# Attention: the order of the gate, sum and context transfers on one DMA queue

## The chip, the cores and the metric

The kernel runs on one core of a Trainium2 chip. The metric is the device time of one execution in microseconds (us), and the median of several runs is given. A profile of one further execution records every instruction on the engines: TensorE (PE, with its weight loads as PEld), VectorE (DVE), ScalarE (ACT) and GpSimd (POOL). It also records the issue of every transfer on SyncE's queue (SP). All the transfers this text speaks of are issued on SP, one after the other.

## The reference

The input x has 128 sequences of 64 tokens and 128 channels, in float32. Four blocks are applied one after the other; three of them hold attention with 16 heads of 8 channels:

```python
def _attend(q, k, v):
    attn = jnp.einsum('bhnd,bhsd->bhns', q, k) * SCALE
    attn = jax.nn.softmax(attn, axis=-1)
    o = jnp.einsum('bhns,bhsd->bhnd', attn, v)
...
x = x + g_sa * (_attend(q, k, v) @ sa_proj_w + sa_proj_b)      # self: gated per sequence
x = x + (_attend(q_, k_, v_) @ ca_proj_w + ca_proj_b)          # cross: keys, values of the context
x = x + g_ff * (gelu(xm @ fc1_w + fc1_b) @ fc2_w + fc2_b)      # MLP
```

Block 0 is self-attention, cross-attention to `ctx_1024` and an MLP. Block 1 is one cross-attention with modulated inputs. Block 2 is again self-attention, cross-attention and an MLP. Block 3 is an attention to 64 prototypes, a router and three experts. Gates, shifts and scales come from `cond_1024`, one row per sequence.

## The kernel before

The tokens are cut into 16 groups of 512 (8 sequences). x stays in SBUF as 16 tiles `xs[s]` of 128 tokens x 4 x 128 channels. There are five attention stages, called L0s and L2s (self), L0c, L1c and L2c (cross). A pair of a stage and a group is an item here, so there are 80 items: 32 of self-attention and 48 of cross-attention. L0s and L0c are one stream of 32 items, and L1c, L2s and L2c are another of 48; between and behind the streams run the MLPs and block 3.

The program order on each engine is written out by hand. `prepare` and `finish` are generators, and `step(k)` advances them by single pieces; each item i has two steps, u = 0 and u = 1, one for each half of its sequences. In a step DVE takes the maxima of the scores (`mx`, L449) and subtracts them (`e`, L451), PE turns the result, ACT takes the exponential (`eT`, L471), PE weighs the values, and ACT copies the outcome into `o` (L492).

`prepare` of an item has eight pieces. The first loads the context tile `c` (256 KB, L363) for a cross item and does nothing for a self item; the later ones make the statistics, the normed input `xn` (POOL), the normed context `cn`, and then keys, queries and values. `step` calls the first piece of item i + 4 at the start of the step with u = 0. In L0c the transposed context is also stored to DRAM (`ctxT`, L385).

`finish` of item j has four pieces:

1. In step (j + 1, u = 1): for a self item, four loads of the gate tiles `gt` (128 KB each, L505); four stores of the rows of `o` that hold the sums of the softmax to DRAM (`sums`, L510); one load `rc` (L515) that brings the sums back spread over 128 partitions; four transfers within SBUF that move half of `o` (L518).
2. In step (j + 2, u = 0): DVE's reciprocal of `rc` (L520), its store to DRAM (`recs`, L522), and the load `rb` (256 KB, L524) that broadcasts it to all channels.
3. In step (j + 2, u = 1): on POOL `oT` = `o` x `rb` (L527) and the addition of the bias to x (L529), which is `gt[1]` for a self item.
4. In step (j + 3, u = 0): the projection `py` on PE (L533), and for a self item `y` = `py` x `gt[0]` on DVE (L538) and its addition to x on POOL (L539); for a cross item one addition on DVE (L535).

SP works through its queue in that order. A transfer that waits for a semaphore holds all those behind it. `rc` waits until `sums` has landed, `recs` waits for the reciprocal, and `rb` waits until `recs` has landed. `o`, `gt` and `rc` have two buffers each, `rb` and `oT` one, `c` three.

Of the kernel before, what the change touches and what calls it, by code (L numbers as in the profile page):

```python
# [9 lines left out]
F32 = mybir.dt.float32  # L10
# [10 lines left out]
NT = TT * P  # L21
# [38 lines left out]
def tile_kernel(ctx: ExitStack, tc: tile.TileContext, a: dict, out: bass.AP):  # L60
    nc = tc.nc
# [4 lines left out]
    def const(shape, name):  # L66
        return cp.tile(shape, F32, tag=name, name=name)
# [38 lines left out]
    for name, n in (("L0_xcond_ca_proj_b", P), ("L1_xcond_bp", P), ("L2_xcond_b_cproj", P), ("L3_xcond_router_b", 3)):  # L106
        t = const([P, n], name)
# [16 lines left out]
    dp = ctx.enter_context(tc.tile_pool(name="dp", bufs=1, space=bass.MemoryType.DRAM))  # L124
# [307 lines left out]
    def scores(pools, at, u):  # L432

        pool, psc = pools[0], pools[2]
        qT, kbd = at["qT"], at["kbd"]

        sc = psc.tile([P, 4, 512], F32, tag="sc", name="sc")
        for t2 in range(2):
            for h in range(2):
                b = 4 * u + 2 * t2 + h  # L440
                for g in range(4):
                    T.matmul(  # L442
                        sc[ts(h, L), g, ts(t2, 256)],
                        qT[ts(g, 32), ts(b, L)],
                        kbd[ts(g, 32), :, b, :],
                        start=True, stop=True,
                    )
        mx = pool.tile([P, 32], F32, tag="mx", name="mx")
        V.tensor_reduce(mx, sc.rearrange("p g (m k) -> p (g m) k", k=L), AX.X, ALU.max)  # L449
        e = pool.tile([P, 32, L], F32, tag="e", name="e")  # L450
        V.tensor_tensor(  # L451
            e, sc.rearrange("p g (m k) -> p (g m) k", k=L),
            mx.unsqueeze(2).broadcast_to([P, 32, L]), ALU.subtract,
        )
        return e

    def turned(pools, e, eT, gg):

        pp = pools[3].tile([P, 2, 512], F32, tag="pt", name="pp")
        e6 = e.rearrange("p (g t i j) k -> p g t i (j k)", g=4, t=2, i=2)
        for g2 in range(2):
            for i in range(2):
                for t2 in range(2):
                    for h in range(2):
                        T.transpose(  # L467
                            pp[:, h, ts(4 * g2 + 2 * i + t2, L)],
                            e6[ts(h, L), 2 * gg + g2, t2, i], ident[ts(h, L), ts(h, L)],
                        )  # L470
        S.activation(eT[:, gg], pp, AF.Exp, scale=HD ** -0.5)  # L471

    def weighted(pools, at, u, eT):


        pool, psum = pools[:2]
        po = psum.tile([P, 2, 256], F32, tag="mm", name="po")
        e7 = eT.rearrange("p a h (g i t q) -> p a h g i t q", g=2, i=2, t=2)

        for i in range(2):  # L480
            for t2 in range(2):
                for h in range(2):
                    for g in range(4):
                        T.matmul(  # L484
                            po[ts(g, 32), i, ts(2 * t2 + h, L)],
                            at["vbd"][:, 4 * u + 2 * t2 + h, 2 * g + i, :],
                            e7[:, g // 2, h, g % 2, i, t2, :],
                            start=True, stop=True,
                        )
        if u == 0:  # L490
            at["o"] = pool.tile([P, 2, NT], F32, tag="o", name="o")
        S.copy(at["o"][:, :, ts(u, 256)], po)  # L492

    def finish(pools, at):

        pool, psum = pools[:2]
        s, o = at["s"], at["o"]
        cross = at["layer"][2] == "c"
        if not cross:
            gt = []  # L500
            for i in range(2):
                t = pool.tile([P, TT, P], F32, tag=f"gt{i}", name="gt")
                for h in range(2):
                    r = gates[at["wp"]][i].rearrange("(s t h) c -> s h t c", t=TT, h=2)[s, h]
                    nc.sync.dma_start(t[ts(h, L)], r.unsqueeze(0).broadcast_to([L, TT, P]))  # L505
                gt.append(t)

        sums = dp.tile([16, NT], F32, tag="sums", name="sums", bufs=2)
        for g in range(4):
            nc.sync.dma_start(  # L510
                sums[ts(g, 4), :].rearrange("(i j) t -> j i t", i=2),
                o[32 * g + 16 : 32 * g + 18, :, :],
            )
        rc = pool.tile([P, L], F32, tag="rc", name="rc")
        nc.sync.dma_start(rc, sums.rearrange("h (c t) -> (h c) t", t=L))  # L515

        for g in range(4):
            nc.sync.dma_start(o[32 * g + 16 : 32 * g + 32, 0, :], o[32 * g : 32 * g + 16, 1, :])  # L518
        yield
        V.reciprocal(rc, rc)  # L520
        recs = dp.tile([16, NT], F32, tag="recs", name="recs", bufs=2)
        nc.sync.dma_start(recs.rearrange("h (c t) -> (h c) t", t=L), rc)  # L522
        rb = pool.tile([P, NT], F32, tag="rb", name="rb", bufs=1)
        nc.sync.dma_start(rb, recs.unsqueeze(1).broadcast_to([16, HD, NT]))  # L524
        yield
        oT = pool.tile([P, NT], F32, tag="oT", name="oT", bufs=1)
        G.tensor_tensor(oT, o[:, 0, :], rb, ALU.mult)  # L527
        bias = proj_bias[at["wp"]].unsqueeze(1).broadcast_to([P, TT, P]) if cross else gt[1]
        G.tensor_tensor(xs[s], xs[s], bias, ALU.add)  # L529
        yield  # L530
        py = psum.tile([P, TT, P], F32, tag="mm", name="py")
        for t in range(TT):
            T.matmul(py[:, t, :], oT[:, ts(t, P)], w[at["wp"]][:, 0], start=True, stop=True)  # L533
        if cross:
            V.tensor_add(xs[s], xs[s], py)  # L535
        else:
            y = pool.tile([P, TT, P], F32, tag="y", name="y")
            V.tensor_tensor(y, py, gt[0], ALU.mult)  # L538
            G.tensor_tensor(xs[s], xs[s], y, ALU.add)  # L539

    def attend(pools, ats):

        n = len(ats)
        prep = [prepare(pools, at) for at in ats]
        fin = [finish(pools, at) for at in ats]

        def go(gens, i):
            if 0 <= i < n:
                next(gens[i], None)

        def ahead(*which):
            for i in which:
                go(prep, i)


        halves = [dict(at=at, u=u) for at in ats for u in range(2)]

        def step(k):
            i, u = divmod(k, 2)
            now, last, past = (  # L560
                halves[k - d] if 0 <= k - d < 2 * n else None for d in range(3)
            )
            if u == 0:
                go(prep, i + 4)
            if now:
                now["e"] = scores(pools, now["at"], now["u"])
            if last:
                last["eT"] = pools[0].tile([P, 2, 2, 512], F32, tag="eT", name="eT")
                turned(pools, last["e"], last["eT"], 0)
            if past:  # L570
                weighted(pools, past["at"], past["u"], past["eT"])
            if u == 0:
                go(fin, i - 2)
                go(prep, i + 1)
                go(fin, i - 3)
            else:
                go(prep, i + 1)
            if last:
                turned(pools, last["e"], last["eT"], 1)
            if u == 0:  # L580
                go(prep, i + 2)
                go(prep, i + 3)
            else:
                go(prep, i + 1)
                go(prep, i + 2)
                go(fin, i - 1)
                go(fin, i - 2)
                go(prep, i + 4)

        return ahead, [lambda k=k: step(k) for k in range(2 * n + 5)]  # L590

    def attention_of(s, layer):
# [628 lines left out]
```

## Time and profile before

| | us |
|---|---|
| median of 3 runs | 1682.3 |
| lowest, highest | 1681.4, 1682.74 |
| the profiled execution | 1678.51 |
| its span, first to last instruction | 1676.7 |
| PE busy | 1598.2 |
| DVE busy | 1287.6 |
| ACT busy | 1030.9 |
| POOL busy | 1069.9 |
| TensorE clock granted, mean share of full | 0.993 |

L0s runs from about 40 to 250 us of the span, L0c to about 430, L1c from about 590 to 790, L2s to about 1000 and L2c to about 1185. A line of a group of instructions gives the line of the kernel, the engine, the operation, output and inputs, and after the first bar the busy time in us and the mean of one in ns; after the second bar stands the idle time of the engine before these instructions, with what ended it behind the arrow. A line of a timeline gives the start and duration in us, the engine and the line; a bracket at its end gives the engine's idle time before it and what ended that. `SPq` is the issue of a transfer by SP's queue, not the transfer itself.

### The profile page before, as it was taken

The numbers are of one execution on the slowest core, as the hardware profiler recorded it, in microseconds if no ns is written. First come the engines' busy times: TensorE is split into PE (matmuls) and PEld (weight loads), VectorE is DVE, ScalarE is ACT, GpSimd is POOL, SyncE is SP. The second block draws the span as 40 slices with busy tenths as digits, with TensorE's granted clock in tenths as the row PEclk, the third lists the DMA queues.
The fourth block names the chain that finished last, engine by engine and source line by source line (L and its number), as shares of the span: only waits on it lengthen the run. The fifth ranks groups of instructions, "written<-read, shape, count | busy, mean of one in ns | idle before, by whom it ended". The sixth has DMA issues, their size and how long they took to land.

```text
span 1676.7 us, 64398 instructions
## 1 busy us (share of the span) xinstructions
PE 1598.2 (95%) x27552; PEld 1071.5 (64%) x27552; DVE 1287.6 (77%) x2426; ACT 1030.9 (61%) x1696; POOL 1069.9 (64%) x1816
## 2 busy tenths in 40 slices
PE   6999989999899899999999899998999999999998
PEld 4666667777554467767767667776555566666665
DVE  6999879999555599999999889998354566666665
ACT  4877757776433578778787778886334444444442
POOL 4777766677699978886778777675745233344322
PEclk8999999999999999999999999999999999999999
DMA  7233333232211012212333332221200011111100
GB/s 218 66 88 80 91 109 96 82 90 63 64 32 54 26 50 65 60 47 54 83 91 88 94 91 66 67 60 46 85 1 7 27 38 39 35 36 38 30 13 16
DMA packets 154812, 104.14 MB, mean 62 GB/s; under 512 B 36069, under 2 KB 133279, under 8 KB 154527
## 3 DMA queue, kind: packets, MB, share of 16 engines
q1 hardware_dynamic: 154320, 100.01, 21.6%
q8 instruction: 216, 3.54, 0.9%
q14 instruction: 69, 0.57, 0.1%
q10 hardware_dynamic: 207, 0.03, 0.0%
HBM read 75.60 MB, written 13.89 MB: 53 GB/s over the span
## 4 chain that ended last, share of the span: by engine, by line
PE 66%; DVE 17%; DMA 6%; SPq 4%; POOL 3%; issue 2%; ACT 2%; POOLq 0%; DVEq 0%; ACTq 0%
PE sc L442 7%; DVE mx L449 7%; DVE e L451 7%; PE pp L467 6%; PE ph L994 6%; PE ph L995 6%; PE ph L651 6%; PE py L657 5%; PE po L484 5%; PE po L1025 5%; PE psT L311 4%; PE py L533 3%; PE pvv L423 3%; PE pq L414 3%; PE pk L401 3%
## 5 line engine op out<-in xcount | busy, mean ns | idle before, releaser
L471 ACT ACTIVATE eT<-pp 128x1024 f32<-128x1024 f32 x320 | 329.6, 1030 | 175.1 <-PE pp L467 174.9
L449 DVE TENSOR_REDUCE mx<-sc 128x32 f32<-128x2048 f32 x160 | 366.1, 2288 | 50.3 <-PE sc L442 50.3
L451 DVE TENSOR_TENSOR e<-sc,mx 128x2048 f32<-128x2048 f32 x160 | 366.7, 2292 | 5.5
L467 PEld LDWEIGHTS pp<-ident,e 64*128 64x128 f32 x5120 | 185.5, 140 | 140.3 <-ACT eT L471 40.8
L467 PE MATMUL pp<-ident,e 64*128 64x64 f32 x5120 | 229.4, 230 | 6.3 <-DVE e L451 4.7
L409 POOL TENSOR_SCALAR kbd<-kT,mask 128x512 f32<-128x512 f32 x318 | 214.5, 693 | 30.1 <-ACT kT L403 27.4
L341 POOL TENSOR_SCALAR xn<-x,nmu,rs 128x128 f32<-128x128 f32 x504 | 220.0, 450 | 13.2
L527 POOL TENSOR_TENSOR oT<-o,rb 128x512 f32<-128x512 f32 x80 | 102.1, 1276 | 189.4 <-DMA rb<-recs 52.5
L442 PE MATMUL sc<-kbd,qT 32*64 32x256 f32 x5120 | 181.9, 391 | 20.6 <-DVE e L451 20.0
L652 ACT ACTIVATE h<-ph,vec 128x512 f32<-128x512 f32 x128 | 87.4, 688 | 158.8 <-PE ph L651 158.7
L484 PE MATMUL po<-eT,vbd 128*32 128x64 f32 x10240 | 177.7, 221 | 4.6 <-DVE y L538 4.0
L1001 ACT ACTIVATE h<-h 128x512 f32<-128x512 f32 x112 | 69.1, 628 | 160.4 <-DVE h L997 130.8
L484 PEld LDWEIGHTS po<-eT,vbd 128*32 128x32 f32 x10240 | 151.4, 110 | 17.6 <-DVE y L538 4.8
L299 POOL TENSOR_TENSOR rs<-rs,nhalf 128x4 f32<-128x4 f32 x128 | 130.4, 1018 | 10.7
L442 PEld LDWEIGHTS sc<-kbd,qT 32*64 32x64 f32 x5120 | 99.4, 132 | 57.0 <-issue 25.1
L997 DVE TENSOR_TENSOR h<-ph,ab 128x512 f32<-128x512 f32 x112 | 76.9, 687 | 64.4 <-PE ph L995 64.3
L492 ACT COPY o<-po 128x512 f32<-128x512 f32 x160 | 95.6, 598 | 28.3 <-POOL oT L527 11.1
L289 DVE BATCH_NORM_STATS2 st<-x 128x6 f32<-128x128 f32 x512 | 110.3, 278 | 0.0
L994 PE MATMUL ph<-nx,w 128*128 128x512 f32 x192 | 99.8, 601 | 0.0
L1018 POOL TENSOR_SCALAR g<-g 128x512 f32<-128x512 f32 x16 | 10.0, 625 | 140.4 <-ACT g L1017 140.4
L1025 PEld LDWEIGHTS po<-w_2o,h 128*128 128x128 f32 x768 | 92.2, 192 | 10.9 <-issue 8.4
L1025 PE MATMUL po<-w_2o,h 128*128 128x128 f32 x768 | 96.4, 275 | 1.8 <-ACT h L1001 1.8
(253 smaller groups left out, 2884.6 us busy)
## 6 DMA issues: line engine op xcount, KB each, us to landing
rb<-recs SPq DMA_DIRECT2D x80, 256.0 KB
c<-in_ctx_dram SPq DMA_DIRECT2D x80, 256.0 KB
o<-o SPq DMA_DIRECT2D x320, 32.0 KB
gt<-gate_L_xcond_sa_proj_w SPq DMA_DIRECT2D x64, 128.0 KB
gt<-gate_L_xcond_W_proj SPq DMA_DIRECT2D x64, 128.0 KB
sums<-o SPq DMA_DIRECT2D x320, 8.0 KB
x<-in_x_dram SPq DMA_DIRECT2D x16, 256.0 KB
ctxT<-cm SPq DMA_DIRECT2D x16, 256.0 KB
```

The lines of the kernel that those rows point to most:

```text
L289: V.bn_stats(st[:, t, :], src[:, t, :])
L299: G.tensor_tensor(rs, rs, nhalf, ALU.pow)
L341: engine.tensor_scalar(xn[:, t, :], src[:, t, :], nmu[:, t : t + 1], rs[:, t : t + 1], ALU.add, ALU.mult)
L409: (V if at.get("first") and j % 2 else G).tensor_scalar(kbd[:, j], by_batch(kT), mask[:, j : j + 1], 1.0, ALU.mult, ALU.mult)
L442: T.matmul(sc[ts(h, L), g, ts(t2, 256)], qT[ts(g, 32), ts(b, L)], kbd[ts(g, 32), :, b, :], start=True, stop=True,)
L449: V.tensor_reduce(mx, sc.rearrange("p g (m k) -> p (g m) k", k=L), AX.X, ALU.max)
L451: V.tensor_tensor(e, sc.rearrange("p g (m k) -> p (g m) k", k=L), mx.unsqueeze(2).broadcast_to([P, 32, L]), ALU.subtract,)
L467: T.transpose(pp[:, h, ts(4 * g2 + 2 * i + t2, L)], e6[ts(h, L), 2 * gg + g2, t2, i], ident[ts(h, L), ts(h, L)],)
L471: S.activation(eT[:, gg], pp, AF.Exp, scale=HD ** -0.5)
L484: T.matmul(po[ts(g, 32), i, ts(2 * t2 + h, L)], at["vbd"][:, 4 * u + 2 * t2 + h, 2 * g + i, :], e7[:, g // 2, h, g % 2, i, t2, :], start=T ...
L994: T.matmul(ps, wn, d["nx"], start=True, stop=False)
L1025: T.matmul(po[:, ex, :], d[q][:, ts(t, P)], k3["w_2o"][:, q, :], start=r == 0, stop=r == 1)
```

## The change

In the first piece of `finish` the four stores of `sums` are issued ahead of the four loads of `gt` instead of behind them; the load `rc` and the rest follow as before. In `step`, the first piece of `prepare` of item i + 4, that is the load of `c`, is called behind the second piece of `finish` of item i - 2 instead of at the start of the step. On SP's queue it then stands behind `recs` and `rb` of that item instead of in front of them. Nothing is added or taken away.

```diff
@@ finish
         cross = at["layer"][2] == "c"
+
+        sums = dp.tile([16, NT], F32, tag="sums", name="sums", bufs=2)
+        for g in range(4):
+            nc.sync.dma_start(
+                sums[ts(g, 4), :].rearrange("(i j) t -> j i t", i=2),
+                o[32 * g + 16 : 32 * g + 18, :, :],
+            )
+
         if not cross:
             gt = []
             for i in range(2):
...
                 gt.append(t)
-
-        sums = dp.tile([16, NT], F32, tag="sums", name="sums", bufs=2)
-        for g in range(4):
-            nc.sync.dma_start(
-                sums[ts(g, 4), :].rearrange("(i j) t -> j i t", i=2),
-                o[32 * g + 16 : 32 * g + 18, :, :],
-            )
         rc = pool.tile([P, L], F32, tag="rc", name="rc")
@@ step
-            if u == 0:
-                go(prep, i + 4)
             if now:
                 now["e"] = scores(pools, now["at"], now["u"])
...
             if u == 0:
                 go(fin, i - 2)
+                go(prep, i + 4)
                 go(prep, i + 1)
                 go(fin, i - 3)
```

## The prediction

> **What bounds the kernel now.** I read the page first: it names the busy engines.
>
> ```profile
> PE 1598.2 (95%) x27552; PEld 1071.5 (64%) x27552; DVE 1287.6 (77%) x2426; ACT 1030.9 (61%) x1696; POOL 1069.9 (64%) x1816
> ```
>
> No share of the whole span decides here, because the change touches only the five attention stages. So I went to the groups of instructions on DVE, first in the window 71 to 250 us (14 items of the first self-attention stage, L0s), then in 785 to 1000 us (L2s).
>
> ```profile
> L520 DVE RECIPROCAL rc<-rc 128x64 f32<-128x64 f32 x14 | 7.7, 551 | 16.7 <-DMA rc<-sums 16.7
> ...
> L520 DVE RECIPROCAL rc<-rc 128x64 f32<-128x64 f32 x17 | 9.3, 549 | 13.5 <-DMA rc<-sums 13.5
> ```
>
> The number after the second bar is idle time of DVE before the group: 16.7 and 13.5 us, all waiting for rc to land. Apart from its waits for PE in front of `mx` (7.1 and 8.8 us) and 1 us before `e`, DVE is never idle in those windows. An item costs DVE 4 x 2.29 (mx, e) + 0.55 + 0.63 (y) + 1.23 (statistics) = 11.6 us, and a self item that does not stall takes 11.9 us from one end of its second o copy to the next (71.45, 83.36, 95.24, 107.13). The stalls are therefore time of the kernel.
>
> Why is rc late? The timeline of SP's queue over one stalled item of L2s shows one closed loop:
>
> ```profile
> 954.43 3.45 SPq L505 DMA_DIRECT2D gt<-gate_L_xcond_W_proj  x4
> 957.97 1.34 SPq L510 DMA_DIRECT2D sums<-o  x4
> 961.06 0.34 SPq L515 DMA_DIRECT2D rc<-sums  x1
> 961.45 2.46 SPq L518 DMA_DIRECT2D o<-o  x4
> 963.95 0.59 SPq L363 DMA_DIRECT2D c<-in_ctx_dram  x1
> 964.58 0.50 SPq L522 DMA_DIRECT2D recs<-rc  x1
> 968.58 0.56 SPq L524 DMA_DIRECT2D rb<-recs  x1
> 969.26 2.88 SPq L505 DMA_DIRECT2D gt<-gate_L_xcond_W_proj  x4
> 972.26 1.31 SPq L510 DMA_DIRECT2D sums<-o  x4
> ```
>
> The columns are start and duration of the issue. The only pauses are two round trips, sums to rc (1.75 us) and recs to rb (3.5 us). ACT and DVE for the same item:
>
> ```profile
> 965.32 0.59 ACT L492 COPY o<-po 128x512 f32<-128x512 f32 x1 [0.28 <-PE po L484]
> ...
> 963.00 0.55 DVE L520 RECIPROCAL rc<-rc 128x64 f32<-128x64 f32 x1 [2.54 <-DMA rc<-sums]
> ...
> 976.83 0.55 DVE L520 RECIPROCAL rc<-rc 128x64 f32<-128x64 f32 x1 [2.23 <-DMA rc<-sums]
> ```
>
> The o that sums reads was ready at 965.91, but sums was issued at 972.26: 6.35 us late, because SP was still waiting for recs and then issued gt. From sums to sums the loop is 14.29 us, more than the 11.9 us of the engines. Where c loads are in the loop (the last six items of L0s and of L2s) the items take 12.8 to 15.8 us from oT to oT. Without them SP needs 11 to 13 us and DVE stalls only now and then.
>
> An item that does not stall, also L2s:
>
> ```profile
> 865.88 0.64 ACT L492 COPY o<-po 128x512 f32<-128x512 f32 x1
> 869.26 1.32 SPq L510 DMA_DIRECT2D sums<-o  x4
> 871.97 0.34 SPq L515 DMA_DIRECT2D rc<-sums  x1
> 873.96 0.54 DVE L520 RECIPROCAL rc<-rc 128x64 f32<-128x64 f32 x1
> ```
>
> From the end of o (866.52) to the place that the reciprocal has in DVE's order is 7.44 us. A chain from o to landed rc that is shorter than this costs DVE nothing.
>
> **The change part by part.**
>
> Gate loads behind sums (32 self items). Nothing is added; four issues of gt (3.0 us for four on average, 2.6 to 3.7) change places with four of sums (1.32 us). SP waits between sums and rc for the sums to land: 1.63 us on average in the self items. Now gt is issued in that wait, so the loop gets shorter by about 1.6 us, and when SP is the late one, sums starts 3.0 us sooner. rc, though, comes behind gt: sums 1.32 + 0.1 + gt 3.0 + 0.1 = 4.5 us after sums starts instead of about 3.0. Net, rc is 1.5 us sooner where SP is late, and up to 1.5 us later where SP has been waiting for o. Queued behind rc on SP are the four o shuffles, recs and rb; all move with it. The consumers of gt, the add on POOL (L529) and y on DVE (L538), come after rb has landed, that is over 13 us after o; gt gets there in about 8.
>
> What rc itself takes when it stands behind 512 KB of gt is not in this trace. Lower bound: 1.67 us from issue to reciprocal, the least now, with nothing in front of it. Upper bound: gt's last load lands as late as the slowest rb (239.45 to oT at 244.41, 4.96 us), and rc with it. rc's issue starts 0.72 us after that load's, so 4.2 us. I take 2.2, near the lower end, because sums stands directly behind gt today and takes only 1.63 us to land against 1.2 us at best without gt (1044.47 to 1045.69): 0.4 us more. The chain is then 4.5 + 2.2 = 6.7 us, inside the 7.44. With gt at 3.7 it is 7.4, still just inside.
>
> The c load behind rb (48 cross items are loaded in this way; 12 of the loads fall in self items). Issue 0.59 us, 256 KB. It stood before recs and now stands behind rb, ahead of the next sums and, in L0c and the end of L0s, ahead of the store ctxT. SP loses no work. From recs to rb the self items take 2.4 to 4.2 us where c stands just before recs (mean 3.1) and mostly 1.76 without c, now and then over 3 (mean 2.3): 0.9 us of the loop. The next sums now stands behind c's data; its landing may take longer (bound below 0, above the 0.9 that c costs recs now), but gt's 3.0 us of issue cover a landing of 1.63 + 0.9. c itself arrives 5 to 6 us later. Its nearest reader, cn of L2c, runs 14.2 us after the issue (1062.04 to 1076.23), so some 8 us are left. In the cross stages the reciprocal does not wait (o end 1043.28 to reciprocal 1051.20 is 7.9 us, and rc, issued at 1045.69, has 5.5 us for a landing of 1.7), and the items run at 12.0 us with PE busy 108.00 of 108.00 us (window 1031 to 1139). There an earlier rb gains nothing. A gain is at most 1 us (13 periods of L0c, 254.84 to 411.82, are 157.0 us against 156.0 at 12.0). A loss needs a sums more than 1.4 us later at the tightest item (rc at 332.11, reciprocal at 335.21), and c can delay it by 0.9. I take 0.
>
> The new loop with c: sums 1.34 + 0.1 + gt 3.0 + 0.1 + rc 0.39 + o 2.82 + recs 0.35 + wait 1.8 + rb 0.68 + c 0.63 = 11.2 us, and 11.8 with ctxT in L0s. It is below 11.9, but in L0s only just.
>
> The sum: DVE's stalls of 16.7 + 13.5 = 30.2 us go, less what comes back where a loop of 11.8 us has a slow issue or a slow landing. I keep 4 us for that (0.35 us for each of 12 items with c). A second count agrees: from the o end of the third item of L0s (71.45) to that of the first of L0c (254.84) are 14 periods, 183.4 us against 166.5 at 11.89; in L2s 805.07 to 994.40 are 15 periods, 189.3 against 178.4. That is 16.9 + 11.0 = 27.9 us, and it includes a granted clock of 0.79 in the window 240 to 250 us, where PE stands idle for 2.68 us before py at 246.34. So 26 us. The profiled execution took 1678.5 us (span 1676.7 and 1.8 around it), 3.8 below the median; 1678.5 - 26 = 1652.5, in terms of the median 1656.
>
> **The rivals.**
>
> Slower: rc held behind gt. It decides from the point where the stall is again the 1.0 us that an item loses now (30.2 us over 30 items): chain 8.44, so rc to reciprocal 3.9 us. At the upper bound of 4.2 us with gt at 3.0 the chain is 8.7, a stall of 1.3, +9 us over 30 items: 1692. For it: 512 KB in 512-byte pieces stand in front. Against it: sums lands 1.63 us after standing in the same place. An intermediate form, in which gt's last load lands like the typical rb (3.5 us from its issue, so rc after 2.8) gives a chain of 7.3 us, and 8.0 with gt at 3.7; a quarter of the items then stall 0.6 us, 4.5 us in all: 1660.
> The Trainium skill, page "DMA: Bandwidth & Descriptors", section "Queues, rings and completion order", says that a DMA's completion count is written only after all earlier writes of the same DMA engine; this speaks against the change, since rc could not be reported before gt has landed. By that rule the intermediate form holds at least; the trace, in which sums follows gt with only 0.4 us more, does not settle it.
>
> Half the gain: the wait moves on to POOL. oT (L527) waits for rb, and ACT's o copy two items on waits for oT; the waits of ACT for oT, those put down to gt among them, are 10.1 us in 71 to 250 and 7.9 in 785 to 1000. If they are a limit of their own and stay, 30.2 - 18 = 12 us are gained: 1670. For it: POOL idles 48.0 us before 17 oT in L2s. Against: these waits stand in the same items as the stalls (973.52 waits 1.86 us), and POOL works only 9.7 us per item (its groups of that window added up).
>
> No change: SP is not the limiter after all, sums waits for o as in L1c, and only the order differs: 1682. The 6.35 us above speak against it.
>
> **How the numbers follow.** Forecast 0.53 (its own range 1648 to 1664: all 30.2 us and a little of the clock, down to 18), the intermediate form 0.20, half the gain 0.14, no change 0.03, slower 0.10. The range 1645 to 1674 takes in the forecast, the intermediate form and most of the half. About 0.2% (3.4 us) is what a measurement of this kernel can tell from no change: faster 0.87, same 0.03, slower 0.10.
>
> **What would show it.** Right: DVE's idle before L520 below 6 us in L0s and L2s together (30.2 now); on SP, gt between sums and rc with no pause before rc; recs to rb near 1.8 us also where cross items are loaded; self items at 11.9 us, cross items at 12.0 as before. Wrong: rc to reciprocal above 2.9 us with DVE waiting for it, sums landing later than gt's issue ends, or ACT's waits before L492 unchanged.

## The result and the profile after

The changed kernel takes 1659.5 us (median of 4 runs, 1655.5 to 1661.2) against 1681.85 us of the kernel before on the same chip: ratio 0.9873, 95% interval 0.9851 to 0.9894. (The ratios in this text are those of the measurement, with its intervals; they are not the quotients of the medians.) Its profiled execution took 1658.35 us, 20.2 less than the one before. A second measurement on another chip gave a ratio of 0.990 (0.9882 to 0.9919). The forecast was 1656, the range 1645 to 1674.

The reciprocal's line moved from L520 to L521. Its groups in the windows 71 to 250 us (L0s and the first items of L0c) and 785 to 1000 us (L2s) of the changed kernel:

```profile
L521 DVE RECIPROCAL rc<-rc 128x64 f32<-128x64 f32 x14 | 7.7, 551 | 7.7 <-DMA rc<-sums 7.6
...
L521 DVE RECIPROCAL rc<-rc 128x64 f32<-128x64 f32 x18 | 9.9, 549 | 5.2 <-DMA rc<-sums 4.9
```

The last figures are DVE's idle time before the reciprocal: 7.7 and 5.2 us, where it was 16.7 and 13.5. The self items got shorter: from the third item of L0s to the first of L0c an item takes 12.19 us instead of 13.10 (14 items, 12.7 us), from the second item of L2s to the first of L2c 12.17 instead of 12.62 (15 items, 6.8 us). Together that is 19.5 of the 20.2 us. The items of L0c and L2c run at 12.01 and 11.95 us, practically as before (12.08 and 11.97).

SP's queue over one item of L2s that loads c, in the changed kernel:

```profile
911.63 0.56 SPq L525 DMA_DIRECT2D rb<-recs  x1
912.24 0.58 SPq L363 DMA_DIRECT2D c<-in_ctx_dram  x1
913.12 1.17 SPq L502 DMA_DIRECT2D sums<-o  x4
914.40 3.65 SPq L513 DMA_DIRECT2D gt<-gate_L_xcond_W_proj  x4
918.22 0.49 SPq L516 DMA_DIRECT2D rc<-sums  x1
918.74 3.04 SPq L519 DMA_DIRECT2D o<-o  x4
922.35 0.35 SPq L523 DMA_DIRECT2D recs<-rc  x1
923.85 0.56 SPq L525 DMA_DIRECT2D rb<-recs  x1
```

And the o copy and the reciprocal of that item:

```profile
912.45 0.65 ACT L492 COPY o<-po 128x512 f32<-128x512 f32 x1
...
921.77 0.55 DVE L521 RECIPROCAL rc<-rc 128x64 f32<-128x64 f32 x1 [1.16 <-DMA rc<-sums]
```

sums now starts at 913.12, as soon as o is there (913.10); in the item shown of before it was 6.35 us late. rc follows gt without a pause, and rb follows recs after 1.50 us. In this item SP is no longer the late one. (In five items of L0s and one of L2s that load c it still is, by 0.7 to 2.7 us.) But rc is landed only 3.5 us after its issue at 918.22, and DVE stood idle for 1.16 us. Over the 15 self items in which DVE still waits, rc to reciprocal has a median of 3.49 us; before, over the 18 that waited, it was 1.79.

### The profile page after: what moved, and what is told of

Same layout as the page of the kernel before. It is cut to its first block, busy times and chain, and to the rows that moved or that the text cites. A ratio compares the mean times of both kernels' runs of the same rounds, so it can differ in the third digit from the quotient of the medians.

```text
span 1656.6 us, 64393 instructions
## 1 busy us (share of the span) xinstructions
PE 1591.8 (96%) x27552; PEld 1069.7 (65%) x27552; DVE 1286.4 (78%) x2426; ACT 1030.7 (62%) x1696; POOL 1068.0 (64%) x1816
## 4 chain that ended last, share of the span: by engine, by line
PE 71%; DVE 18%; DMA 4%; POOL 2%; issue 2%; SPq 1%; ACT 1%; POOLq 0%; DVEq 0%; ACTq 0%
PE sc L442 8%; PE pp L467 7%; DVE e L451 7%; DVE mx L449 7%; PE ph L651 6%; PE py L657 6%; PE ph L994 6%; PE po L484 6%; PE ph L995 6%; PE po L1025 5%; PE psT L311 5%; PE py L534 3%; PE pk L401 3%; PE pvv L423 3%; PE pq L414 3%; DMA rc<-sums 2%
## 5 line engine op out<-in xcount | busy, mean ns | idle before, releaser
L1030 DVE SCALAR_TENSOR_TENSOR acc<-po,pr,acc 128x128 f32<-128x128 f32 x192 | 67.2, 350 | 40.2 <-PE po L1025 35.6
```

## The experiments

Theory A: both parts shorten SP's loop, each by its own term, and what is left of the stalls is rc, which lands late because the gate tiles' data stand in front of it. Rivals: the place of c is worth nothing (B); what is left is SP still being late at sums (C); or the saved time only moves to the waits for oT (D).

**One part alone.** e1 takes the c load back to where it was and keeps the gates behind sums; e2 does the opposite.

```diff
 # e1, from the changed kernel
+            if u == 0:
+                go(prep, i + 4)
             if now:
...
                 go(fin, i - 2)
-                go(prep, i + 4)
                 go(prep, i + 1)
```

> The gate loads stand behind sums as in the changed kernel, the c load stands ahead of recs as before. Theory A (both parts shorten SP's loop, each by its own term: 1.6 us for the gates, 0.9 us for c): where c loads are, the loop is 12.1 us in L2s and 12.7 us with ctxT in L0s instead of 11.2 and 11.8, so the 12 self items that load c stall about 0.5 us more each; 1665 us, recs to rb back at about 3.1 us in these items, idle of DVE before the reciprocal in L0s and L2s together about 18 us (12.5 in the changed kernel, 30.2 before). Rival B (the place of c is worth nothing, the gates did it all): 1660 us, the same idle as in the changed kernel.

> The c load stands behind rb as in the changed kernel, the gate loads stand ahead of sums as before. Theory A: recs to rb falls to about 2.0 us, the loop of the self items that load c from 14.1 to 13.2 us, so of their 23 us of stalls about 11 go, and the 7 us of the other self items stay; 1671 us. Rival B: c moves its delay from recs to the next sums, nothing is gained: 1681 us. If the two parts simply add, this gain and that of the gates alone give the 22 us of the whole change.

e1 took 1667.4 us, ratio 0.9878 (0.9824 to 0.9931); e2 took 1677.3 us, ratio 0.9946 (0.9924 to 0.9969), both against 1684.5 us on that chip. The reciprocal's groups, from about 40 to 250 and 780 to 1010 us, first of e1:

```profile
L521 DVE RECIPROCAL rc<-rc 128x64 f32<-128x64 f32 x16 | 8.8, 551 | 10.8 <-DMA rc<-sums 10.8
...
L521 DVE RECIPROCAL rc<-rc 128x64 f32<-128x64 f32 x19 | 10.4, 548 | 9.0 <-DMA rc<-sums 8.9
```

and of e2:

```profile
L520 DVE RECIPROCAL rc<-rc 128x64 f32<-128x64 f32 x16 | 8.8, 550 | 15.6 <-DMA rc<-sums 15.5
...
L520 DVE RECIPROCAL rc<-rc 128x64 f32<-128x64 f32 x19 | 10.4, 548 | 12.8 <-DMA rc<-sums 12.8
```

With c back in front, 19.8 us of idle are there instead of 12.9, and recs to rb in the items that load c takes 3.18 us on average, as before the change (3.13); in the changed kernel it is 2.12. So B falls, by the idle time and by e2, whose interval lies clear of no gain; e1's time alone could not tell, since its ratio (0.9878) is that of the whole change (0.9873). The gains of the parts in the medians, 17.0 and 7.2 us, make 24 us, near the 22 of the whole, but the intervals are too wide to show that the parts add up, and the stalls do not: 10.4 us go with the gates alone and 1.8 with c alone, 17.3 with both. e2's stalls fell less than A asked (11 us; its time, 7 us against 11, leaves that open): recs to rb did get 0.8 us shorter (2.34), but with the gates still in front, SP comes to sums 4.7 us late in those items (5.0 before), and the stalls there fall only from 23.2 to 20.7 us. The 0.8 us are a small part of a loop that stays the bound. With the gates out of the way the place of c is worth 6.9 us of stalls (19.8 to 12.9).

**Half of the gates elsewhere.** e3 leaves `gt[1]` (256 KB) between sums and rc and loads `gt[0]` behind recs, while SP waits for recs to land anyway.

```diff
-            for i in range(2): ... four gate loads
+            load_gate(1)
...
         nc.sync.dma_start(recs.rearrange("h (c t) -> (h c) t", t=L), rc)
+        if not cross:
+            load_gate(0)
         rb = pool.tile([P, NT], F32, tag="rb", name="rb", bufs=1)
```

> The changed kernel, but only gt[1] (256 KB) stands between sums and rc; gt[0] (256 KB) stands between recs and rb, in the wait for recs to land. Theory A (what is left of the stalls is rc landing late behind the 512 KB of gt, 3.3 to 4.2 us after its issue): rc to landing about 2.6 us, the chain from o to landed rc 5.4 to 6 us, no stall left; idle before the reciprocal below 2 us in L0s and L2s together, 1649 us. Rival C (what is left is SP being late at sums, as in items 11 to 15): those go too because the loop is 1.4 us shorter, but the stalls of items whose sums was on time (5.7 of the 12.5 us) stay: 1653 us. Rival D (rb lands so late behind gt[0] that oT and with it ACT's o copy wait): oT over 5 us after rb's issue, 1660 us or more.

It took 1655.8 us, ratio 0.9813 (0.9768 to 0.9858), an interval that holds the times of both A and C. DVE's idle before the reciprocal is 0.0 us in both stages. The changed kernel and the split were then run side by side on a third chip:

> The changed kernel once more, beside the split on the same chip. Theory A and C alike: 0.985 to 0.989 of the kernel before.

> The split once more, beside the changed kernel on the same chip. If the stalls that are left in the changed kernel (12.5 us before the reciprocal in its first profile) were time of the kernel, the split is faster than it by 4 to 12 us. If that time only moves to another wait, the two are equal.

Against 1677.3 us there, the changed kernel took 1660.8 us (0.990, 0.9882 to 0.9919, a little less gain than the 0.985 to 0.989 expected) and the split 1654.0 us (0.9858, 0.984 to 0.9876): 6.8 us faster. The reciprocal of the split in the windows 71 to 226 and 785 to 957 us of that run, and its SP queue over one item:

```profile
L524 DVE RECIPROCAL rc<-rc 128x64 f32<-128x64 f32 x13 | 7.0, 541 | 0.0
...
L524 DVE RECIPROCAL rc<-rc 128x64 f32<-128x64 f32 x14 | 7.6, 542 | 0.0
```

```profile
903.63 0.35 SPq L526 DMA_DIRECT2D recs<-rc  x1
904.02 1.29 SPq L513 DMA_DIRECT2D gt<-gate_L_xcond_W_proj  x2
905.42 0.55 SPq L530 DMA_DIRECT2D rb<-recs  x1
906.01 0.59 SPq L363 DMA_DIRECT2D c<-in_ctx_dram  x1
907.55 1.17 SPq L502 DMA_DIRECT2D sums<-o  x4
908.81 1.63 SPq L513 DMA_DIRECT2D gt<-gate_L_xcond_W_proj  x2
910.62 0.47 SPq L519 DMA_DIRECT2D rc<-sums  x1
```

Both round trips now have a pair of gate loads in them, rb is issued 1.4 us after recs is out in this item, and no self item waits for rc, neither the on-time ones nor those where sums is late. So C falls: by it the 5.7 us of the items with a timely sums would have stayed. And where c is loaded, sums is still 0.6 us late on average (0.9 to 1.0 in the changed kernel), and 1.7 to 2.0 us in the last three items of L0s, without a stall. D does not hold either: oT comes 14.2 to 14.9 us after o, in the changed kernel 14.1 to 15.4, and 4.0 to 4.2 us on average after rb's issue, not over 5.

The split shortens the chain from sums to landed rc in two places. rc is issued 3.0 us after sums instead of 4.4, because two issues fewer stand between; and by the trace's completion records (the times at which a transfer reports its landing) it lands about 3.0 us after its issue instead of 3.4 (medians), because less data stands in front. The earlier issue is the larger part.

Were the stalls that were left time of the kernel? About half of them. In the second run of the changed kernel they came to 14.8 us, of which the split gains 6.8. The other half comes back one step later, as DVE's wait for PE's scores in front of `mx`. These are its groups from the third item of L0s to the first of L0c and from the second item of L2s to the first of L2c, first of the changed kernel (71.5 to 241.3 and 793.0 to 977.1 us of its second run):

```profile
L449 DVE TENSOR_REDUCE mx<-sc 128x32 f32<-128x2048 f32 x28 | 64.1, 2288 | 6.1 <-PE sc L442 6.0
...
L449 DVE TENSOR_REDUCE mx<-sc 128x32 f32<-128x2048 f32 x31 | 70.9, 2288 | 7.0 <-PE sc L442 7.0
```

and of the split (71.4 to 237.6 and 788.0 to 968.3 us):

```profile
L449 DVE TENSOR_REDUCE mx<-sc 128x32 f32<-128x2048 f32 x28 | 64.2, 2291 | 8.9 <-PE sc L442 8.9
...
L449 DVE TENSOR_REDUCE mx<-sc 128x32 f32<-128x2048 f32 x30 | 68.8, 2292 | 11.2 <-PE sc L442 11.2
```

Over these 29 items the idle before the reciprocal falls by 13.5 us, that before `mx` grows by 7.0, and the items get 7.3 us shorter.

**No gates in the loop.** e7 loads the gate tiles of the first group in each self stage and uses them for all groups.

```diff
-            gt = []
+            gt = kept_gates.get(at["wp"])
+            if gt is None:
+                gt = kept_gates[at["wp"]] = [] ... four gate loads, once
```

> The changed kernel, but the gate tiles of group 0 are loaded once in each self stage and used for all its groups; 30 of the 32 sets of gate loads are left out (the gates of the other groups are wrong by that). Theory A (rc lands late because of gt's data in front of it): rc is there 1.7 to 1.9 us after its issue, the chain from o is 4.5 us, SP's loop 8.5 us, no stall, and the time is the split's within 2 us, since DVE at 11.9 us per item is then the bound of both. If the gate traffic costs something besides SP's order (SBUF, DMA engines), this is faster than the split by more than 3 us.

It took 1652.15 us, ratio 0.985 (0.9835 to 0.9865) on the chip where the split took 1654.0. DVE's idle before the reciprocal is 0.3 and 0.0 us. By the completion records rc lands 1.9 us after its issue (median of the 32 self items), where it takes 3.4 in the changed kernel. So the split has recovered all but about 2 us of what the gate loads can cost, as A asked (its own four runs spread over 5 us); the self items run at 11.9 to 12.0 us in both, the period of an item without a stall.

**What holds rc.** e8 puts the four o shuffles ahead of rc, so that gt's data have some 3 us more to drain.

```diff
-        rc = pool.tile(...); nc.sync.dma_start(rc, sums...)
         for g in range(4):
             nc.sync.dma_start(o[32 * g + 16 : 32 * g + 32, 0, :], o[32 * g : 32 * g + 16, 1, :])
+        rc = pool.tile(...); nc.sync.dma_start(rc, sums...)
         yield
```

> The changed kernel, but the four o shuffles stand ahead of rc. 2.5 to 3.5 us then lie between gt's last issue and rc's. Theory A (rc is held by gt's data as long as they are in the DMA engines): rc to reciprocal falls from 3.5 to below 2.4 us where DVE waits; the chain is 1.2 + 2.9 + 2.8 + 2.2 = 9 us, so every self item stalls by 1.2 to 1.6 us: idle before the reciprocal 35 to 50 us in L0s and L2s together, 1685 to 1700 us. If rc takes 3.5 us for a reason of its own (its place behind sums, DRAM), the chain is 10.4 us and the idle 80 us or more, 1730 us.

The single run took 1712.4 us. One self item of L2s, on SP and DVE (its o was ready at 903.11):

```profile
903.13 1.16 SPq L502 DMA_DIRECT2D sums<-o  x4
904.38 2.60 SPq L513 DMA_DIRECT2D gt<-gate_L_xcond_W_proj  x4
907.03 2.91 SPq L516 DMA_DIRECT2D o<-o  x4
910.28 0.35 SPq L518 DMA_DIRECT2D rc<-sums  x1
...
912.21 0.55 DVE L521 RECIPROCAL rc<-rc 128x64 f32<-128x64 f32 x1 [1.21 <-DMA rc<-sums]
```

rc is there 1.93 us after its issue; the median over the 32 self items, all of which stall, is 1.95. Behind gt directly it was 3.49. What holds rc is therefore gt's data, and not its place behind sums. The time is above the 1685 to 1700 us expected: the idle in L0s and L2s was 55.7 us, more than 35 to 50, and the cross stages, which the expectation left out, stall 32 us (7.3 before the change), since their rc is later by the shuffles too.

The Trainium skill, page "DMA: Bandwidth & Descriptors", section "Queues, rings and completion order", has a DMA's completion written only after all earlier writes of the same DMA engine. By that rule rc cannot be reported before gt has landed, and the trace agrees: 3.49 us behind 512 KB of gt, 1.95 once they had drained. In the changed kernel the last of rc's completions comes at least 0.15 us after the last of gt's in all 32 self items.

The packet records of the changed kernel show that it is more than a late report: rc's pieces themselves wait behind gt's. rc moves in 128 pieces of 256 bytes and tells its landing by sixteen completions. In the item shown above (rc issued at 918.22) 120 pieces have started by 1.8 us after the issue; the last eight start at 2.7 to 2.9, directly behind the last 512-byte piece of gt. In 26 of the 32 self items the last piece of rc starts within 0.3 us after the last of gt (in the other six 0.8 to 1.3; why is open). And it is one share that is late: the fifteenth completion comes 2.5 us after the issue (median), the last 3.4.

**The gates behind rc.** If rc suffers behind gt, gt could stand behind rc.

```diff
+        rc = pool.tile(...); nc.sync.dma_start(rc, sums...)
         if not cross:
             ... four gate loads
-        rc = pool.tile(...); nc.sync.dma_start(rc, sums...)
```

> The changed kernel, but the four gate loads stand behind rc instead of ahead of it. Theory A: rc, with nothing in front of it, is there 1.7 us after its issue, and no item whose sums is on time stalls; in exchange SP pauses 1.2 to 1.5 us for sums again, so the loop is 12.0 us, 12.6 with c and ctxT, and the items that load c have a late sums and stall as the loop asks: 1656 us. If the o shuffle and recs are held by gt's data as rc is in the changed kernel (2 us), the loop is 14 us and the time 1675 us.

It took 1687.4 us, ratio 1.0018 (0.9992 to 1.0044): the whole gain is gone, and neither guess of the expectation, 1656 or 1675, holds, although rc was landed 1.66 to 1.90 us after its issue wherever DVE waited, as expected, and the reciprocal hardly stalls. Its groups (40 to 250 and 780 to 1010 us), and ACT's waits in 71 to 239 and 797 to 1003 us (waiting engine, line, releaser, total, times, longest):

```profile
L522 DVE RECIPROCAL rc<-rc 128x64 f32<-128x64 f32 x16 | 8.7, 545 | 4.8 <-DMA rc<-sums 4.6
...
L522 DVE RECIPROCAL rc<-rc 128x64 f32<-128x64 f32 x18 | 9.8, 544 | 0.9 <-DMA rc<-sums 0.8
```

```profile
ACT o L492 <- POOL oT L529: 11.3, 8, 2.5
...
ACT o L492 <- POOL oT L529: 12.9, 10, 2.2
```

The gate loads now lie between rc and the o shuffles, recs cannot go out before both are issued, and oT runs 16.4 us after o in the self items without c and 18.5 in those with it (14.1 and 15.4 in the changed kernel). ACT's next o copy needs the buffer that oT reads, so it waits 24 us in all, PE waits for ACT, and DVE for PE: its idle before `mx` is 40.2 us over the same 29 items (16.0 before the change, 13.3 in the changed kernel), and the self items take 12.9 us. This is the mechanism of the rival "half the gain" of the prediction, which the changed kernel escapes (ACT waits 0.5 us for oT in 71 to 230 us), carried to the full. The second guess of the expectation, a loop of 14 us, is seen in part: in the items that load c it is 13.5 us on average from sums to sums, and sums comes 2.6 us after o there (0.9 in the changed kernel). How much of the loss is SP's loop and how much the buffer of o was not separated.

## Why the prediction was right

- **SP's loop as the bound of the self items.** Right. With sums issued first, its mean lateness behind o fell from 5.0 to 0.9 us where c is loaded and from 2.8 to 0.03 elsewhere (the first item of each stage left out). The gain lies in the self items, and in those with c most: their stalls fell from 23.2 to 8.2 us. The new loop was put too short, though: 11.8 us were forecast for the end of L0s, and in its last four items sums follows sums after 12.1 to 13.0 us. So SP is still late there, and the items with a late sums hold 6.8 us of the stalls that are left.
- **gt covers the wait for sums.** Right: 0.1 to 0.2 us lie between gt's last issue and rc.
- **rc behind gt.** This is the term that was mis-sized. I took 2.2 us, near the lower bound of 1.67, and it measured 3.49, inside the bounds and nearer to the upper 4.2. The chain from o to landed rc is then 4.1 + 3.5 = 7.6 us against a place in DVE's order at 7.44: stalls of 0.2 to 1.2 us come back in nine items whose sums is on time, 5.7 us in all. The row I chose by was the wrong one: sums also stood behind gt, but the last of its four issues starts about 1 us after gt's last, and its landing did not wait for all of gt. By the completion records of the kernel before, gt's last load lands later than sums in 15 of the 32 self items. The row to take was gt's own landing, 3.7 us after its last issue there (median) and 3.8 in the changed kernel: rc, issued 0.8 us after that, would by this estimate be there some 3 us after its own issue. I kept 4 us of stalls, and 12.9 are left; this is the intermediate form to which I gave 0.20, whose price was 1660.
- **c behind rb.** Right in size: recs to rb 2.12 us instead of 3.13, predicted 0.9 less, measured 1.0. No reader of c became late, and the items of the cross stages kept their period of 12.0 us.
- **The sum.** 26 us were forecast and 22.3 measured in the medians. Of the 30.2 us of stalls 17.3 went. Beyond them 2.9 us of the profiled gain remain. Most of them stand in L0s, whose items got 12.7 us shorter for 9.0 us of stalls (in L2s 6.8 for 8.3): DVE's wait for PE before `mx` fell there as well, from 8.7 to 5.5 us over the same 14 items (in L2s it rose from 7.3 to 7.8). Before the change (71.45 to 254.84 us) and after it (71.4 to 242.05 us):

```profile
L449 DVE TENSOR_REDUCE mx<-sc 128x32 f32<-128x2048 f32 x28 | 64.1, 2291 | 8.7 <-PE sc L442 8.6
...
L449 DVE TENSOR_REDUCE mx<-sc 128x32 f32<-128x2048 f32 x28 | 64.1, 2288 | 5.5 <-PE sc L442 5.4
```

The granted clock may have a part in it: over these items its mean was 0.97 before and 1.00 after. How much that is worth is not shown. That the total came nearer to the forecast than its main term did is luck: the stalls gave 17.3 us where 26 were counted on, this wait, which the sum does not hold, gave most of the 2.9, and the medians lie 2.1 us further apart than the two profiled executions.

- **Of the signs named ahead**, idle before the reciprocal below 6 us was not met (12.9), and rc to reciprocal above 2.9 us with DVE waiting did occur; recs to rb near 1.8 us with c was nearly met (2.12); self items are at 11.9 where they don't stall.

## What to carry to other kernels

When a queue that issues all transfers in order has become the loop, put independent issues into its round trips, since the wait is paid anyway; but only as many as the trip has room for, in time of issue and in data, because the transfer that closes the trip stands behind them. Two waits with half the filler each were better here than one with all of it. To price a transfer that will stand behind others, take the landing of those others, not that of a neighbour in the queue. And follow the chain beyond the stall that you see: gates behind rc removed the visible stall and lost the same time further on, at a buffer two items later and in a longer loop.

## What was not expected of the hardware

- A load of 32 KB that takes 1.7 to 1.95 us from its issue to its reader takes 3.49 us when four loads of 128 KB, in pieces of 512 bytes, were issued right before it. Of its sixteen completions the last is over 0.5 us later than the fifteenth in 22 of the 32 self items.
- sums issues faster in front of gt than behind it: 1.18 us for four instead of 1.32. rc's own issue takes 0.49 us behind gt, now and then 1.2 to 1.6, instead of 0.34.
